# Fixed issue order, rescaling by halves with the third product two halves later, and splits dealt out, in a bilinear pair kernel

## The chip, the cores and the metric

The kernel runs on one core of one Trainium2 chip. Times are microseconds (us) of device time for one execution; the median of several runs is quoted. Engines are named as in the profile: PE is TensorE (matmuls), PEld its weight loads, DVE is VectorE, ACT is ScalarE, POOL is GpSimd, SP is SyncE, which issues the transfers.

## The reference

For each of the 496 pairs i < j of 32 fields, a 1024 x 128 slice of the input is multiplied by its own 128 x 128 matrix, and the result is multiplied element by element with field j:

```python
v_i = inputs[:, I_IDX, :]          # inputs: 1024 x 32 x 128, fp32
v_j = inputs[:, J_IDX, :]
transformed = jnp.einsum('bpd,ped->bpe', v_i, W)   # W: 496 x 128 x 128
return transformed * v_j           # 1024 x 496 x 128, fp32: 260 MB to write
```

## The kernel before

A pair's result stands in one PSUM tile of 128 x 1024 fp32, with two halves of 512 columns. Each half is one bank of PSUM (point (4) of the prediction's part on the Trainium skill). The first 15 pairs use plain fp32 matmuls. For the other 481, weights and inputs are split into a high and a low part, and the result is put together from three faster products: two are summed in PSUM (`wh*xh`, `wl*xl`; the *first products* below), ScalarE rescales the sum in place, and the *third product* (`wd*xd`) is added on top. VectorE then multiplies by field j, and SyncE sends the output tile off.

```python
LAG = 2
ppool = ctx.enter_context(tc.tile_pool(name="ps", bufs=4, space=bass.MemoryType.PSUM))
...
for q in range(NQ + LAG):
    if q < NQ:
        ...   # at the start of a group of four pairs: load weights, split weights two groups ahead
        ...   # at the start of a field: load an x, split the next field's x
        po[q] = ppool.tile([P, BT], F32, tag="po", name=f"po_{q}")
        ...
            for t in (0, 1):
                for h in range(0, BT, HB):
                    nc.tensor.matmul(po[q][:, h : h + HB], w_s[c][t][:, r], x_s[i][t][:, h : h + HB],
                                     start=t == 0, stop=t == 1)
            nc.scalar.mul(po[q], po[q], 1.0 + EPS)      # both halves at once
    if q >= LAG:
        ...   # third products of pair q - LAG, both halves
        ...   # VectorE's product of the whole pair, and the output's transfer
```

The layer that builds the program inserts all semaphore waits by itself. In the kernel before it also sorts each engine's instructions by its own estimate of time, so the order in the source is only a wish.

A split of four pairs' weights is one ScalarE instruction and three GpSimd ones (3.2 us on GpSimd); a split of half a field's x is the same.

Of the kernel before, what the change touches and what calls it, by code (L numbers as in the profile page):

```python
# [1 line left out]

# [4 lines left out]

F32 = mybir.dt.float32
F32R = mybir.dt.float32r
ALU = mybir.AluOpType  # L10

P = 128
NF = 32
NQ = NF * (NF - 1) // 2
BT = 1024
HB = 512
WC = 4
EPS = 2.0**-12
NATIVE = 5
LAG = 2  # L20


def _pairs():

    return [(i, j) for i in range(NF - 2, -1, -1) for j in range(i + 1, NF)]


@with_exitstack
def kernel(
    ctx: ExitStack,  # L30
    tc: tile.TileContext,
    xt: bass.AP,
    wt: bass.AP,
    out: bass.AP,
):
















    nc = tc.nc
    pairs = _pairs()
    nchunk = NQ // WC

    xpool = ctx.enter_context(tc.tile_pool(name="x", bufs=1))
    spool = ctx.enter_context(tc.tile_pool(name="xs", bufs=2))
    rpool = ctx.enter_context(tc.tile_pool(name="wr", bufs=4))
    wpool = ctx.enter_context(tc.tile_pool(name="ws", bufs=3))
    tpool = ctx.enter_context(tc.tile_pool(name="tmp", bufs=2))  # L60
    opool = ctx.enter_context(tc.tile_pool(name="o", bufs=6))
    ppool = ctx.enter_context(tc.tile_pool(name="ps", bufs=4, space=bass.MemoryType.PSUM))

    x_sb = {}

    def load_x(f, pieces=1):
        x_sb[f] = xpool.tile([P, BT], F32, tag=f"x{f}", name=f"x_{f}")
        s = BT // pieces
        for k in range(pieces):
            nc.sync.dma_start(out=x_sb[f][:, k * s : (k + 1) * s], in_=xt[:, f, k * s : (k + 1) * s])  # L70

    w_raw = {}

    def load_w(c, splits=(0, WC)):
        w_raw[c] = rpool.tile([P, WC, P], F32, tag="w", name=f"w_{c}")
        for a, b in zip(splits, splits[1:]):
            nc.sync.dma_start(out=w_raw[c][:, a:b, :], in_=wt[:, c * WC + a : c * WC + b, :])

    w_s = {}

    def split_w(c):

        raw = w_raw[c].rearrange("p q e -> p (q e)")
        h, l, d = [wpool.tile([P, WC * P], F32R, tag=t, name=f"{t}_{c}") for t in ("wh", "wl", "wd")]
        hs = tpool.tile([P, WC * P], F32, tag="t", name=f"whs_{c}")
        nc.scalar.mul(h, raw, 1.0 - 2.0**-13)  # L86
        nc.gpsimd.tensor_tensor(l, raw, h.bitcast(F32), ALU.subtract)  # L87
        nc.gpsimd.tensor_scalar(hs, h.bitcast(F32), EPS, 1.0, ALU.mult, ALU.mult)  # L88
        nc.gpsimd.tensor_tensor(d, l.bitcast(F32), hs, ALU.subtract)  # L89
        w_s[c] = (h, l, d)  # L90

    x_s = {}

    def split_x(f):

        h, l, d = [spool.tile([P, BT], F32R, tag=t, name=f"{t}_{f}") for t in ("xh", "xl", "xd")]
        for a in range(0, BT, HB):
            s = slice(a, a + HB)
            ls = tpool.tile([P, HB], F32, tag="t", name=f"xls_{f}_{a}")
            nc.scalar.mul(h[:, s], x_sb[f][:, s], 1.0 - 2.0**-13)  # L100
            nc.gpsimd.tensor_tensor(ls, x_sb[f][:, s], h[:, s].bitcast(F32), ALU.subtract)  # L101
            nc.gpsimd.tensor_scalar(l[:, s], ls, 1.0 / EPS, 1.0, ALU.mult, ALU.mult)  # L102
            nc.gpsimd.tensor_tensor(d[:, s], h[:, s].bitcast(F32), l[:, s].bitcast(F32), ALU.subtract)  # L103
        x_s[f] = (h, l, d)

    nq0 = NATIVE * (NATIVE + 1) // 2
    c0 = nq0 // WC

    load_w(0, (0, 1, WC))
    load_x(NF - 2, 2)  # L110
    load_x(NF - 1, 2)
    load_x(NF - 3)
    load_w(1)
    for f in (NF - 4, NF - 5):
        load_x(f)
    load_w(2)

    out_v = out.rearrange("q e b -> q e b")
    po = {}

    def finish(q):
        j = pairs[q][1]
        ot = opool.tile([P, BT], F32, tag="ot", name=f"ot_{q}")
        pieces = 2 if q >= NQ - 2 else 1
        s0 = BT // pieces
        for k in range(pieces):
            s = slice(k * s0, (k + 1) * s0)
            nc.vector.tensor_tensor(ot[:, s], po[q][:, s], x_sb[j][:, s], ALU.mult)  # L128
            nc.sync.dma_start(out=out_v[q, :, s], in_=ot[:, s])

    def second(q):
        i, _ = pairs[q]
        r = slice(q % WC * P, (q % WC + 1) * P)
        for h in range(0, BT, HB):
            nc.tensor.matmul(  # L135
                po[q][:, h : h + HB], w_s[q // WC][2][:, r], x_s[i][2][:, h : h + HB], start=False, stop=True,
                skip_group_check=True,
            )

    for q in range(NQ + LAG):  # L140
        if q < NQ:
            i, j = pairs[q]
            c = q // WC
            if q % WC == 0:
                if c + 3 < nchunk:
                    load_w(c + 3)
                for k in ([c + 2] if c > 0 else [0, 1, 2]):
                    if c0 <= k < nchunk:
                        split_w(k)
            if j == i + 1:  # L150
                for f in ([i - 4] if i < NF - 2 else [NF - 6]):
                    if f >= 0:
                        load_x(f)
                if 0 <= i - 1 < NF - 1 - NATIVE:
                    split_x(i - 1)
            po[q] = ppool.tile([P, BT], F32, tag="po", name=f"po_{q}")
            if q < nq0:
                for h in range(0, BT, HB):
                    nc.tensor.matmul(  # L159
                        po[q][:, h : h + HB],  # L160
                        w_raw[c][:, q % WC, :],
                        x_sb[i][:, h : h + HB],
                        start=True,
                        stop=True,
                    )
            else:
                r = slice(q % WC * P, (q % WC + 1) * P)
                for t in (0, 1):
                    for h in range(0, BT, HB):
                        nc.tensor.matmul(  # L170
                            po[q][:, h : h + HB],
                            w_s[c][t][:, r],
                            x_s[i][t][:, h : h + HB],
                            start=t == 0,
                            stop=t == 1,
                        )
                nc.scalar.mul(po[q], po[q], 1.0 + EPS)  # L177
        if q >= LAG:
            if q - LAG >= nq0:
                second(q - LAG)  # L180
            finish(q - LAG)


# [25 lines left out]
```

## Time and profile before

| | before |
|---|---|
| median of 4 runs | 898.5 us |
| span of the profiled run | 896.0 us |
| TensorE busy | 761.1 us, 85% |
| VectorE, ScalarE, GpSimd busy | 607.0, 558.2, 549.5 us |
| mean transfer rate | 346 GB/s |
| time per pair, 896 / 496 | 1.81 us |

Busy shares do not say who sets the pace; the waits and the order of time do. The lines are in the prediction below.

### The profile page before, as it was taken

How to read it: one execution, taken by the hardware profiler on the slowest of the kernel's cores; microseconds unless marked ns; L12 is line 12 of the kernel's file. 1: busy time of each engine (PE TensorE's matmuls, PEld its weight loads, DVE VectorE, ACT ScalarE, POOL GpSimd, SP SyncE). 2: the span in 40 equal slices, each digit the busy share in tenths (PEclk: the TensorE clock that was granted, in tenths of full speed). 3: DMA queues.
4: the chain of work that ended last, by engine and by line, in shares of the span. 5: the costliest groups of instructions: out<-in, count | busy, mean ns of one | idle time of the engine just before them, and what ended most of it. 6: DMA issues, size and time to landing. Idle time of an engine off the chain costs nothing.

```text
span 896.0 us, 10407 instructions
## 1 busy us (share of the span) xinstructions
PE 761.1 (85%) x2946; PEld 526.2 (59%) x2946; DVE 607.0 (68%) x498; ACT 558.2 (62%) x655; POOL 549.5 (61%) x523
## 2 busy tenths in 40 slices
PE   7988888888888888888888888888888888898887
PEld 2455555555666565555565666655656566665665
DVE  3666666666777666676676767776667777677766
ACT  2266666666676566566665667665756666666565
POOL 1878877777666774664747565665655647474441
PEclk9999999999999999999999999999999999999999
DMA  8999999899999898998998999998998899999997
GB/s 329 416 340 370 360 355 343 318 361 338 376 357 362 332 370 327 339 361 320 353 343 336 343 363 356 355 352 321 355 341 334 336 339 330 343 345 339 337 342 304
DMA packets 94666, 310.03 MB, mean 346 GB/s; under 512 B 10513, under 2 KB 10769, under 8 KB 94609
## 3 DMA queue, kind: packets, MB, share of 16 engines
q1 hardware_dynamic: 94608, 309.37, 92.3%
q8 instruction: 23, 0.38, 0.2%
q14 instruction: 35, 0.28, 0.1%
HBM read 49.28 MB, written 260.05 MB: 345 GB/s over the span
## 4 chain that ended last, share of the span: by engine, by line
PE 32%; ACT 25%; issue 19%; POOL 11%; DMA 1%; DVE 0%; POOLq 0%; ACTq 0%; DVEq 0%
ACT po L177 20%; PE po L170 17%; PE po L135 14%; ACT wh L86 4%; POOL wl L87 4%; POOL wd L89 4%; POOL whs L88 2%; DMA out_dram<-ot 1%; ACT xh L100 1%; POOL xls L101 1%; DVE ot L128 0%; POOL xl L102 0%; POOLq L87 0%; ACTq L177 0%; POOL xd L103 0%
## 5 line engine op out<-in xcount | busy, mean ns | idle before, releaser
L128 DVE TENSOR_TENSOR ot<-po,x 128x1024 f32<-128x1024 f32 (+1 forms) x498 | 607.0, 1220 | 285.4 <-ACT po L177 141.7
L177 ACT ACTIVATE po<-po 128x1024 f32<-128x1024 f32 x481 | 476.9, 1009 | 298.5 <-PE po L170 298.5
L135 PE MATMUL po<-xd,wd 128*128 128x512 f32 x962 | 325.7, 420 | 123.8 <-ACT po L177 123.0
L87 POOL TENSOR_TENSOR wl<-w,wh 128x512 fp32r<-128x512 f32 x121 | 154.5, 1277 | 301.7 <-ACT wh L86 301.7
L135 PEld LDWEIGHTS po<-xd,wd 128*128 128x128 f32 x962 | 152.7, 188 | 257.5 <-ACT po L177 162.8
L170 PE MATMUL po<-xh,wh 128*128 128x512 f32 x962 | 300.9, 394 | 0.0
L170 PE MATMUL po<-xl,wl 128*128 128x512 f32 x962 | 298.1, 391 | 0.0
L170 PEld LDWEIGHTS po<-xl,wl 128*128 128x128 f32 x962 | 180.6, 188 | 42.2
L170 PEld LDWEIGHTS po<-xh,wh 128*128 128x128 f32 x962 | 180.6, 188 | 42.1 <-issue 0.5
L89 POOL TENSOR_TENSOR wd<-wl,whs 128x512 fp32r<-128x512 f32 x121 | 156.6, 1294 | 7.9
L86 ACT ACTIVATE wh<-w 128x512 fp32r<-128x512 f32 x121 | 75.5, 624 | 19.3 <-DMA w<-in_wt_dram 19.3
L88 POOL TENSOR_SCALAR whs<-wh 128x512 f32<-128x512 f32 x121 | 75.1, 621 | 10.2
L101 POOL TENSOR_TENSOR xls<-x,xh 128x512 f32<-128x512 f32 x52 | 67.4, 1296 | 4.2
L103 POOL TENSOR_TENSOR xd<-xh,xl 128x512 fp32r<-128x512 f32 x52 | 66.9, 1287 | 2.2
L100 ACT ACTIVATE xh<-x 128x512 fp32r<-128x512 f32 x52 | 32.1, 621 | 13.6 <-PE po L170 8.7
L102 POOL TENSOR_SCALAR xl<-xls 128x512 fp32r<-128x512 f32 x52 | 32.4, 623 | 4.4
L159 PE MATMUL po<-x,w 128*128 128x512 f32 x60 | 29.6, 656 | 6.2 <-DMA x<-in_xt_dram 6.2
L159 PEld LDWEIGHTS po<-x,w 128*128 128x128 f32 x60 | 12.3, 209 | 22.6 <-issue 21.6
L86 ACT ACT_TABLE_LOAD x1 | 1.3, 1283 | 0.7 <-PEq L196 0.7
L196 POOL MEMSET const-float32-0.0<- 128x1 f32 x1 | 0.1, 99 | 0.2 <-issue 0.2
L196 POOL MEMSET const-bfloat16-1.0<- 128x1 bf16 x1 | 0.1, 102 | 0.0
L196 POOL MEMSET const-uint8-127<- 128x1 uint8 x1 | 0.1, 102 | 0.0
(1 smaller groups left out, 0.1 us busy)
## 6 DMA issues: line engine op xcount, KB each, us to landing
out_dram<-ot SPq DMA_DIRECT2D x494, 512.0 KB, 3.8
w<-in_wt_dram SPq DMA_DIRECT2D x123, 256.0 KB, 3.9
x<-in_xt_dram SPq DMA_DIRECT2D x30, 512.0 KB, 6.0
x<-in_xt_dram SPq DMA_DIRECT2D x4, 256.0 KB, 4.4
out_dram<-ot SPq DMA_DIRECT2D x4, 256.0 KB, 2.6
w<-in_wt_dram SPq DMA_DIRECT2D x1, 192.0 KB, 2.6
w<-in_wt_dram SPq DMA_DIRECT2D x1, 64.0 KB, 1.8
```

What stands on the lines that cost most here:

```text
L86: nc.scalar.mul(h, raw, 1.0 - 2.0**-13)
L87: nc.gpsimd.tensor_tensor(l, raw, h.bitcast(F32), ALU.subtract)
L88: nc.gpsimd.tensor_scalar(hs, h.bitcast(F32), EPS, 1.0, ALU.mult, ALU.mult)
L89: nc.gpsimd.tensor_tensor(d, l.bitcast(F32), hs, ALU.subtract)
L100: nc.scalar.mul(h[:, s], x_sb[f][:, s], 1.0 - 2.0**-13)
L101: nc.gpsimd.tensor_tensor(ls, x_sb[f][:, s], h[:, s].bitcast(F32), ALU.subtract)
L103: nc.gpsimd.tensor_tensor(d[:, s], h[:, s].bitcast(F32), l[:, s].bitcast(F32), ALU.subtract)
L128: nc.vector.tensor_tensor(ot[:, s], po[q][:, s], x_sb[j][:, s], ALU.mult)
L135: nc.tensor.matmul(po[q][:, h : h + HB], w_s[q // WC][2][:, r], x_s[i][2][:, h : h + HB], start=False, stop=True, skip_group_check=True,)
L159: nc.tensor.matmul(po[q][:, h : h + HB], w_raw[c][:, q % WC, :], x_sb[i][:, h : h + HB], start=True, stop=True,)
L170: nc.tensor.matmul(po[q][:, h : h + HB], w_s[c][t][:, r], x_s[i][t][:, h : h + HB], start=t == 0, stop=t == 1,)
L177: nc.scalar.mul(po[q], po[q], 1.0 + EPS)
```

## The change

Its intent is to end the turns that TensorE and ScalarE take. One context manager fixes each engine's order as the source has it. The unit becomes half a pair: two products of half u, its rescaling, then the third product of half u - 2. VectorE still multiplies whole pairs. Splits are put on a list with an earliest and a latest pair, and at most one is issued per pair. Output tiles go from 6 to 5, raw weight tiles from 4 to 5, and the first two x tiles are issued from ScalarE.

```diff
+    ctx.enter_context(tc.manual_schedule())
+    def first(u):
+        q, h = divmod(u, 2)
+        ...
+        s = slice(h * HB, (h + 1) * HB)
+        if h == 0:
+            po[q] = ppool.tile([P, BT], F32, tag="po", name=f"po_{q}")
+        ...
+            for t in (0, 1):
+                nc.tensor.matmul(po[q][:, s], w_s[c][t][:, r], x_s[i][t][:, s], start=t == 0, stop=t == 1)
+            nc.scalar.mul(po[q][:, s], po[q][:, s], 1.0 + EPS)
+    def second(u):
+        ...
+            nc.tensor.matmul(
+                po[q][:, s], w_s[q // WC][2][:, r], x_s[i][2][:, s], start=False, stop=True, skip_group_check=True
             )
+        ...
+        elif h == 1:
+            nc.vector.tensor_tensor(ots[q], po.pop(q), x_sb[j], ALU.mult)
+            nc.sync.dma_start(out=out[q], in_=ots[q])
+    for u in range(2 * NQ + LAG):
+        ...
+            first(u)
+        if u >= LAG:
+            second(u - LAG)
+        if u % 2 == 1:
+            ready = [t for t in todo if t[0] <= q]
+            if ready:
+                ready[0][2]()
+                todo.remove(ready[0])
```

(The removed lines are those of the kernel before, above.)

More of the change, by code (lines that the diff above doesn't have):

```diff
@@ L20 @@
 LAG = 2
+WLEAD = 4
+XLEAD = 3
 def _pairs():
@@ L57, with load_x @@
     spool = ctx.enter_context(tc.tile_pool(name="xs", bufs=2))
-    rpool = ctx.enter_context(tc.tile_pool(name="wr", bufs=4))
+    rpool = ctx.enter_context(tc.tile_pool(name="wr", bufs=5))
     wpool = ctx.enter_context(tc.tile_pool(name="ws", bufs=3))
     tpool = ctx.enter_context(tc.tile_pool(name="tmp", bufs=2))
-    opool = ctx.enter_context(tc.tile_pool(name="o", bufs=6))
+    opool = ctx.enter_context(tc.tile_pool(name="o", bufs=5))
     ppool = ctx.enter_context(tc.tile_pool(name="ps", bufs=4, space=bass.MemoryType.PSUM))
     x_sb = {}
-    def load_x(f, pieces=1):
+    def load_x(f, pieces=1, eng=None):
         x_sb[f] = xpool.tile([P, BT], F32, tag=f"x{f}", name=f"x_{f}")
@@ L69, in load_x @@
         for k in range(pieces):
-            nc.sync.dma_start(out=x_sb[f][:, k * s : (k + 1) * s], in_=xt[:, f, k * s : (k + 1) * s])
+            (eng or nc.sync).dma_start(out=x_sb[f][:, k * s : (k + 1) * s], in_=xt[:, f, k * s : (k + 1) * s])
     w_raw = {}
@@ L92, with split_x @@
     x_s = {}
-    def split_x(f):
-        h, l, d = [spool.tile([P, BT], F32R, tag=t, name=f"{t}_{f}") for t in ("xh", "xl", "xd")]
-        for a in range(0, BT, HB):
-            s = slice(a, a + HB)
-            ls = tpool.tile([P, HB], F32, tag="t", name=f"xls_{f}_{a}")
-            nc.scalar.mul(h[:, s], x_sb[f][:, s], 1.0 - 2.0**-13)
-            nc.gpsimd.tensor_tensor(ls, x_sb[f][:, s], h[:, s].bitcast(F32), ALU.subtract)
-            nc.gpsimd.tensor_scalar(l[:, s], ls, 1.0 / EPS, 1.0, ALU.mult, ALU.mult)
-            nc.gpsimd.tensor_tensor(d[:, s], h[:, s].bitcast(F32), l[:, s].bitcast(F32), ALU.subtract)
-        x_s[f] = (h, l, d)
+    def split_x(f, a):
+        if a == 0:
+            x_s[f] = [spool.tile([P, BT], F32R, tag=t, name=f"{t}_{f}") for t in ("xh", "xl", "xd")]
+        s = slice(a, a + HB)
+        h, l, d = [t[:, s] for t in x_s[f]]
+        ls = tpool.tile([P, HB], F32, tag="t", name=f"xls_{f}_{a}")
+        nc.scalar.mul(h, x_sb[f][:, s], 1.0 - 2.0**-13)
+        nc.gpsimd.tensor_tensor(ls, x_sb[f][:, s], h.bitcast(F32), ALU.subtract)
+        nc.gpsimd.tensor_scalar(l, ls, 1.0 / EPS, 1.0, ALU.mult, ALU.mult)
+        nc.gpsimd.tensor_tensor(d, h.bitcast(F32), l.bitcast(F32), ALU.subtract)
@@ L106 @@
     nq0 = NATIVE * (NATIVE + 1) // 2
     c0 = nq0 // WC
+    first_q = {i: q for q, (i, j) in reversed(list(enumerate(pairs)))}
+    todo = []
+    for c in range(c0, nchunk):
+        todo.append(((c - 2) * WC + 1, max(c * WC, nq0), lambda c=c: split_w(c)))
+    for i in range(NF - 2 - NATIVE, -1, -1):
+        for a in range(0, BT, HB):
+            todo.append((first_q[i + 1] + 1 if i < NF - 3 - NATIVE else 2, first_q[i], lambda i=i, a=a: split_x(i, a)))
+    todo.sort(key=lambda t: t[1])
     load_w(0, (0, 1, WC))
-    load_x(NF - 2, 2)
@@ L111 @@
-    load_x(NF - 1, 2)
+    load_x(NF - 2, 2, nc.scalar)
+    load_x(NF - 1, 2, nc.scalar)
     load_x(NF - 3)
     load_w(1)
-    for f in (NF - 4, NF - 5):
+    for f in range(NF - 4, NF - 4 - XLEAD, -1):
         load_x(f)
-    load_w(2)
-    out_v = out.rearrange("q e b -> q e b")
-    po = {}
-    def finish(q):
-        j = pairs[q][1]
-        ot = opool.tile([P, BT], F32, tag="ot", name=f"ot_{q}")
-        pieces = 2 if q >= NQ - 2 else 1
-        s0 = BT // pieces
-        for k in range(pieces):
-            s = slice(k * s0, (k + 1) * s0)
-            nc.vector.tensor_tensor(ot[:, s], po[q][:, s], x_sb[j][:, s], ALU.mult)
-            nc.sync.dma_start(out=out_v[q, :, s], in_=ot[:, s])
@@ L131, in second @@
-    def second(q):
-        i, _ = pairs[q]
-        r = slice(q % WC * P, (q % WC + 1) * P)
-        for h in range(0, BT, HB):
+    for c in range(2, WLEAD):
+        load_w(c)
+    ctx.enter_context(tc.manual_schedule())
+    po, ots = {}, {}
+    def first(u):
+        q, h = divmod(u, 2)
+        i, c = pairs[q][0], q // WC
+        r = slice(q % WC * P, (q % WC + 1) * P)
+        s = slice(h * HB, (h + 1) * HB)
+        if h == 0:
+            po[q] = ppool.tile([P, BT], F32, tag="po", name=f"po_{q}")
+        if q < nq0:
+            nc.tensor.matmul(po[q][:, s], w_raw[c][:, q % WC, :], x_sb[i][:, s], start=True, stop=True)
+        else:
+            for t in (0, 1):
+                nc.tensor.matmul(po[q][:, s], w_s[c][t][:, r], x_s[i][t][:, s], start=t == 0, stop=t == 1)
+            nc.scalar.mul(po[q][:, s], po[q][:, s], 1.0 + EPS)
@@ L135, in second @@
+    def second(u):
+        q, h = divmod(u, 2)
+        i, j = pairs[q]
+        r = slice(q % WC * P, (q % WC + 1) * P)
+        s = slice(h * HB, (h + 1) * HB)
+        if q >= nq0:
             nc.tensor.matmul(
-                po[q][:, h : h + HB], w_s[q // WC][2][:, r], x_s[i][2][:, h : h + HB], start=False, stop=True,
-                skip_group_check=True,
-            )
-    for q in range(NQ + LAG):
-        if q < NQ:
-            i, j = pairs[q]
-            c = q // WC
-            if q % WC == 0:
-                if c + 3 < nchunk:
-                    load_w(c + 3)
-                for k in ([c + 2] if c > 0 else [0, 1, 2]):
-                    if c0 <= k < nchunk:
-                        split_w(k)
-            if j == i + 1:
-                for f in ([i - 4] if i < NF - 2 else [NF - 6]):
-                    if f >= 0:
-                        load_x(f)
-                if 0 <= i - 1 < NF - 1 - NATIVE:
-                    split_x(i - 1)
-            po[q] = ppool.tile([P, BT], F32, tag="po", name=f"po_{q}")
-            if q < nq0:
-                for h in range(0, BT, HB):
-                    nc.tensor.matmul(
-                        po[q][:, h : h + HB],
-                        w_raw[c][:, q % WC, :],
-                        x_sb[i][:, h : h + HB],
-                        start=True,
-                        stop=True,
-                    )
-            else:
-                r = slice(q % WC * P, (q % WC + 1) * P)
-                for t in (0, 1):
-                    for h in range(0, BT, HB):
-                        nc.tensor.matmul(
-                            po[q][:, h : h + HB],
-                            w_s[c][t][:, r],
-                            x_s[i][t][:, h : h + HB],
-                            start=t == 0,
-                            stop=t == 1,
-                        )
-                nc.scalar.mul(po[q], po[q], 1.0 + EPS)
-        if q >= LAG:
-            if q - LAG >= nq0:
-                second(q - LAG)
-            finish(q - LAG)
@@ new lines, in second @@
+                po[q][:, s], w_s[q // WC][2][:, r], x_s[i][2][:, s], start=False, stop=True, skip_group_check=True
+            )
+        if h == 0:
+            ots[q] = opool.tile([P, BT], F32, tag="ot", name=f"ot_{q}")
+        if q >= NQ - 2:
+            nc.vector.tensor_tensor(ots[q][:, s], po[q][:, s], x_sb[j][:, s], ALU.mult)
+            nc.sync.dma_start(out=out[q, :, s], in_=ots[q][:, s])
+        elif h == 1:
+            nc.vector.tensor_tensor(ots[q], po.pop(q), x_sb[j], ALU.mult)
+            nc.sync.dma_start(out=out[q], in_=ots[q])
@@ new lines @@
+    for u in range(2 * NQ + LAG):
+        q = u // 2
+        if u % (2 * WC) == 0 and q // WC + WLEAD < nchunk:
+            load_w(q // WC + WLEAD)
+        if u < 2 * NQ:
+            i, j = pairs[q]
+            if u % 2 == 0 and j == i + 1 and 0 <= i - 2 - XLEAD:
+                load_x(i - 2 - XLEAD)
+            first(u)
[6 more added lines that the diff above has]
+                todo.remove(ready[0])
@@ L184 @@
+    assert not todo
 def kernel(**inputs):
```

## The prediction

> **What bounds the kernel now.** I read the page's busy table first, for the engine nearest to its limit, then the waits of every engine, then the order of time within four pairs, and last the DMA rate in stretches where the queue was full.
>
> ```profile
> PE 761.1 (85%) x2946; PEld 526.2 (59%) x2946; DVE 607.0 (68%) x498; ACT 558.2 (62%) x655; POOL 549.5 (61%) x523
> ...
> q1 hardware_dynamic: 94608, 309.37, 92.3%
> ```
>
> No engine is full. The DMA engines look it at 92%, but that is the time that packets were under way; the bytes decide, below. PE's 761 us is not solid either, because ends of matmuls are modelled. From the starts in the trace, two neighbouring 512-column matmuls lie 232 ns apart (median), so the six of a pair need 6 x 0.232 = 1.39 us. A pair takes 896 / 496 = 1.81 us. Who waits for whom:
>
> ```profile
> ACT po L177 <- PE po L170: 298.5, 237, 7.8
> PEld po L135 <- ACT po L177: 162.8, 195, 1.7
> DVE ot L128 <- ACT po L177: 141.7, 89, 1.6
> PE po L135 <- ACT po L177: 123.0, 245, 1.2
> ```
>
> TensorE waits for ScalarE's rescaling of the pair, and ScalarE waits for TensorE: they take turns. The order of time shows how:
>
> ```profile
> 402.34 0.62 PE L170 MATMUL po<-xh,wh 128*128 128x512 f32 x2
> 402.80 0.62 PE L170 MATMUL po<-xl,wl 128*128 128x512 f32 x2
> ...
> 403.26 0.62 PE L170 MATMUL po<-xh,wh 128*128 128x512 f32 x2
> 403.46 1.01 ACT L177 ACTIVATE po<-po 128x1024 f32<-128x1024 f32 x1 [1.75 <-PE po L170]
> 403.72 0.61 PE L170 MATMUL po<-xl,wl 128*128 128x512 f32 x2
> 404.38 0.62 ACT L86 ACTIVATE wh<-w 128x512 fp32r<-128x512 f32 x1
> 404.52 0.73 PE L135 MATMUL po<-xd,wd 128*128 128x512 f32 x2 [0.19 <-ACT po L177]
> ...
> 404.91 1.02 ACT L177 ACTIVATE po<-po 128x1024 f32<-128x1024 f32 x1
> ...
> 405.97 0.74 PE L135 MATMUL po<-xd,wd 128*128 128x512 f32 x2 [0.72 <-ACT po L177]
> ...
> 406.55 0.62 PE L170 MATMUL po<-xh,wh 128*128 128x512 f32 x2
> ```
>
> The source asks for a lag of two pairs, but the built order here is the first two products of pairs A and B, then the third products of A and B at once. TensorE therefore waits for A's rescaling, and for B's behind a weight split (404.38) that sits between the two. Eight first products, four third ones and their waits take 406.55 - 402.34 = 4.21 us instead of 2.78. This comes once in each group of four pairs: of the 497 gaps between starts of VectorE's products, 334 lie between 1.35 and 1.50 us (TensorE's own pace), and 125 between 2.4 and 3.0, beside 121 weight splits. The long ones cost about 125 x (2.82 - 1.40) = 178 us. Summing TensorE's start-to-start gaps beyond the normal 232 ns gives 203 us, of which 187 are before third products.
>
> Then the transfers:
>
> ```profile
> 20.00:40.00 20.00, 19.75 (x53) 9.58 (x51) 13.48 (x11) 4.38 (x7) 16.97 (x17) 1.00 1.03 417
> 180.00:190.00 10.00, 8.39 (x35) 5.84 (x34) 7.41 (x7) 6.59 (x8) 9.50 (x10) 1.00 1.03 417
> 300.00:400.00 100.00, 85.57 (x338) 60.02 (x338) 68.31 (x56) 63.79 (x76) 62.40 (x60) 1.00 0.92 343
> 430.00:440.00 10.00, 8.40 (x34) 5.83 (x34) 7.58 (x7) 6.27 (x8) 9.50 (x10) 1.00 1.03 418
> ```
>
> The last column is GB/s. With enough outputs outstanding the queue moves 417, also in 1 us slices with no load under way and two to four outputs outstanding (419). On average it moves 346. So a share of 0.92 hides a sixth of spare rate, and the kernel is bound by the turns of TensorE and ScalarE, with the DMA limit 17% below.
>
> **What the Trainium skill says.** (1) "ScalarE: Activation LUTs", section "What ACT_TABLE_LOAD costs": an ACTIVATE with immediate scale takes 186 ns + 0.833 ns per element, and neighbours overlap by about 93 ns. The trace agrees closely: 624 ns at 512 columns (613 by the formula), 1009 at 1024 in PSUM (1039), and two of the latter back to back take 1.93 us, 0.09 less than twice one. (2) "DMA: Bandwidth & Descriptors", "Specifications": 435 GB/s at the fabric, about 358 from HBM for each core. The trace holds 417 for 20 us, so 358 is not the limit on this core. (3) "TensorE: Matmul & The Clock Gate", the table at its head: matmuls keep program order and ScalarE's queue is strictly first in, first out, so an instruction placed badly holds all behind it. The split at 404.38 does just that. (4) "PSUM — Partial Sum Buffer", "Terms": a bank holds 512 fp32, so half of a pair is one bank, and ScalarE can rescale one while TensorE writes the other. No run shows that yet.
>
> **The change, part by part.** *Half-wise work, third product two halves later.* TensorE does two matmuls of half u, then the third of u-2. After the first two of u end, five matmuls pass (u+1's two, u-1's third, u+2's two) before u's third: 5 x 0.232 = 1.16 us. A half's rescaling is estimated at 1.009 - 512 x 0.833 ns = 0.58, at most 0.62 as in the splits. So 0.5 us of slack is left in every half, and the 187 us of waits before third products should go. One split (0.62) in front delays a half to about 0.1 us before or after its deadline, and the surplus of 0.70 - 0.58 per half recovers that.
>
> *Price on ScalarE.* 481 rescalings of 1009 ns become 962 of about 0.60: 577 instead of 477 us; with splits (75.5 + 32.1) 685 us less overlaps of up to 0.09 each. Per pair at most 1.42 us: it comes near TensorE's 1.39 but lies beside it.
>
> *VectorE by whole pairs*: as before, 1.22 us per pair. *Splits dealt out*, at most one per pair, about seven pairs ahead: the same 173 GpSimd jobs of some 3.2 us, 549 us in all, off the path except early, where the groups of the first field are short: 7 to 9 pairs need four jobs, 12.7 us, and TensorE takes 10 to 13. I expect 2 to 5 us of waits there and at the first weight splits.
>
> *Start*: two x tiles are issued from ScalarE while SyncE issues the rest; before, TensorE sat 1.60 us waiting for the third tile and DMA moved only 216 GB/s between 4 and 6 us. Gain 2 to 3 us. *Outputs 6 to 5 buffers*: four can be in flight while VectorE fills one, enough for the full rate seen with three. *Raw weights 4 to 5, one chunk more lead*: no cost on the path.
>
> The sum: TensorE alone would end at 30 (native pairs, 15 x 1.71 from 4.5) + 481 x 1.39 + 5 of tail = 704 us. Bytes: 310.03 MB / 0.417 = 743, plus 2.5 us before the first byte and about 3 of ramp and landing at the end: 749. The transfers take over as the bound: 1.50 us per pair on average, 1.45 late, where each field's x serves more pairs. TensorE and ScalarE lie so close to it (1.39, 1.42) that jitter will not be absorbed wholly by five output tiles and four PSUM tiles; I add 1%, 8 us. So 757 us, 141 less.
>
> **The rivals.** *A: five outputs starve the DMA.* An output lands 3.5 us (median) after issue, up to 5.5 when full; five slots at 1.5 us allow 7.5 per round: 1.22 for VectorE, 0.4 for the issue, 5.8 in flight. It fits; if it did not, some 1.6 us per pair, about 800. *B: ScalarE becomes the bound* through strict order: a split that waits for a raw weight, or a rescaling of 0.62 and no overlap, gives 1.46 plus waits, about 765 to 790. For it: 92% busy. Against: raw weights are loaded seven pairs before their split. *C: halves serialise*, if TensorE's write of one half had to wait for ScalarE's of the other in the same tile. Then each pair would gain two waits of some 0.6 us: 900 to 1000. Against: the second half of the first x tile is waited for separately in the trace (1.05 us before the third native weight load), so dependencies are kept by region. *D: the DMA doesn't hold 417 over the whole run* with mostly writes; at 400, 780. Nothing in the saturated stretches hints at it.
>
> **Range and chances.** The floor of 743 to 749 from bytes is hard, so the low end is 740; A, B or D half true give 795. Only C, or an unforeseen stall in the fixed order, would keep the time near 898. Faster by over 2%: 0.96; within 2%: 0.03; slower: 0.01.
>
> **What would show it.** Right: DMA near 410 to 418 GB/s in nearly all slices; VectorE waiting for output tiles to land; waits of third products for ScalarE nearly gone; gaps between VectorE starts around 1.45 to 1.55 without the group at 2.8; ScalarE near 670 us busy with halves at 0.58 to 0.62. Wrong: DMA below 390 with TensorE waiting for ScalarE (B), for PSUM (C), or VectorE waiting for landings at a DMA rate well under 417 (A, D).

## The result, and the profile after

| | before | changed |
|---|---|---|
| median of 4 runs | 898.5 us | 1116.9 us |
| ratio, 95% interval | | 1.2435 (1.2414 to 1.2457) |
| span | 896.0 us | 1114.9 us |
| mean transfer rate | 346 GB/s | 278 GB/s |

Ratios are the mean time of one kernel's runs over that of the other's in the same rounds, so they differ a little from the quotient of the medians. The change made the kernel 24% slower.

In the changed kernel L148 holds the first products, L149 the rescaling, L157 the third product and L166 VectorE's; in other runs these numbers shift by a few lines. From its page, the busy times, the transfers and two groups (mean ns of one after the busy us, then idle time before them and what ended it):

```profile
PE 954.5 (86%) x2946; PEld 515.9 (46%) x2946; DVE 607.6 (54%) x498; ACT 637.9 (57%) x1136; POOL 549.3 (49%) x523
...
q1 hardware_dynamic: 94032, 308.32, 73.1%
...
L149 ACT ACTIVATE po<-po 128x512 f32<-128x512 f32 x962 | 560.9, 583 | 452.0 <-PE po L148 431.7
L148 PE MATMUL po<-xh,wh 128*128 128x512 f32 x962 | 430.6, 448 | 121.1 <-ACT po L149 86.8
```

The transfers, which should have become the bound, are emptier than before. ScalarE is busy 80 us longer, as the halves cost, but idle 43% of the time: so it is not simply overloaded. TensorE's busy time rose although it does the same 2946 matmuls: a record lasts 0.39 to 0.50 us, its end is modelled, and in a stream with a pitch of 0.23 us records overlap, while the last one before a wait counts in full. The waits of the changed kernel, in us in total, times, longest:

```profile
ACT po L149 <- PE po L148: 431.7, 478, 10.4
PEld po L148 <- ACT po L149: 272.2, 481, 1.1
PEld po L157 <- ACT po L149: 172.2, 364, 0.8
PE po L148 <- ACT po L149: 86.8, 167, 0.7
```

Before, of TensorE's work only third products waited for ScalarE in the list. Now L148 does, the *first* products, 481 times: once in each pair, and never in the design. In order of time, one pair's period (start, duration, what; in brackets the idle time before it and what ended it):

```profile
406.20 0.19 PEld L148 LDWEIGHTS po<-xh,wh 128*128 128x128 f32 x1 [0.45 <-ACT po L149]
406.20 0.51 PE L148 MATMUL po<-xh,wh 128*128 128x512 f32 x1
...
406.55 0.39 PE L148 MATMUL po<-xl,wl 128*128 128x512 f32 x1
...
406.77 0.39 PE L157 MATMUL po<-xd,wd 128*128 128x512 f32 x1
...
407.00 0.39 PE L148 MATMUL po<-xh,wh 128*128 128x512 f32 x1
...
407.03 1.20 ACT L149 ACTIVATE po<-po 128x512 f32<-128x512 f32 x2 [0.88 <-PE po L148]
...
407.23 0.39 PE L148 MATMUL po<-xl,wl 128*128 128x512 f32 x1
407.67 0.19 PEld L157 LDWEIGHTS po<-xd,wd 128*128 128x128 f32 x1 [0.47 <-ACT po L149]
...
408.29 0.19 PEld L148 LDWEIGHTS po<-xh,wh 128*128 128x128 f32 x1 [0.43 <-ACT po L149]
```

At 406.20 TensorE starts the second half of pair q, then (406.77) a third product of q - 1, then the first half of q + 1 (407.00, 407.23). The last of these is over at 407.62. ScalarE's two rescalings, of q's second half and q + 1's first, end at 408.23. Only at 408.29 do the products of q + 1's second half begin. They write another bank, but they waited for that rescaling. The loop adds up: 407.23 - 406.20 = 1.03 for four starts, 0.39 for the last matmul to its end, about 0.60 for one rescaling, 0.06 to the restart: 2.08 us, against 1.39 without waits.

The built program says the same. Of pair 144, its instructions with the waits that the build put on them (a listing, not the profile; h0 and h1 are the halves; a wait is shown by the instruction that it waits for):

```
PE   first  h0   waits for VectorE's product of pair 140 (the tile's last user)
ACT  scale  h0   waits for PE first h0
PE   first  h1   waits for ACT scale h0      <- another bank, same tile
ACT  scale  h1   waits for ACT scale h0 (and for PE first h1)
PE   third  h0   waits for ACT scale h1      <- another bank, same tile
DVE  whole pair  waits for PE third h1
```

Both marked waits are between instructions that touch different halves. In the build used here, dependencies in a PSUM tile are kept by the whole tile. The listing is not kept with the runs, but the semaphores in the traces agree: the first weight load of a second half carries a wait on ScalarE's semaphore in all 481 pairs of the changed kernel, in 2 of e1 (a tile for each half) and in 1 of e3 (one rescaling for each pair).

Of the gaps between VectorE's starts, 312 average 2.10 us and 171 average 2.49; from the 21st product on, each of the 165 long ones holds exactly one of ScalarE's 173 splits, and the short ones none. A split thus adds 0.39 us to the loop, in front of the rescaling that TensorE waits for. 312 x 2.10 + 171 x 2.49 = 1081 of the 1115 us; the rest is the start and the plain fp32 pairs.

### The profile page after: what moved, and what is told of

The parts are those of the page before. It is cut to its first block, busy times and chain, and to the rows that moved or that the text cites. A ratio compares the mean times of both kernels' runs of the same rounds, so it can differ in the third digit from the quotient of the medians.

```text
span 1114.9 us, 11346 instructions
## 1 busy us (share of the span) xinstructions
PE 954.5 (86%) x2946; PEld 515.9 (46%) x2946; DVE 607.6 (54%) x498; ACT 637.9 (57%) x1136; POOL 549.3 (49%) x523
## 4 chain that ended last, share of the span: by engine, by line
PE 53%; ACT 34%; issue 10%; DMA 2%; ACTq 0%; DVE 0%; SPq 0%
PE po L148 44%; ACT po L149 25%; PE po L157 7%; ACT wh L88 6%; ACT xh L103 3%; PE po L145 2%; DMA x<-in_xt_dram 1%; DMA out_dram<-ot 1%; ACTq L149 0%; DVE ot L166 0%; SPq L167 0%; DVE ot L163 0%; SPq L79 0%
## 5 line engine op out<-in xcount | busy, mean ns | idle before, releaser
L166 DVE TENSOR_TENSOR ot<-po,x 128x1024 f32<-128x1024 f32 x494 | 604.9, 1225 | 503.1 <-PE po L157 484.2
L149 ACT ACTIVATE po<-po 128x512 f32<-128x512 f32 x962 | 560.9, 583 | 452.0 <-PE po L148 431.7
L148 PE MATMUL po<-xh,wh 128*128 128x512 f32 x962 | 430.6, 448 | 121.1 <-ACT po L149 86.8
L157 PE MATMUL po<-xd,wd 128*128 128x512 f32 x962 | 426.2, 443 | 30.6 <-ACT po L149 1.8
L148 PE MATMUL po<-xl,wl 128*128 128x512 f32 x962 | 380.0, 395 | 0.0
L148 PEld LDWEIGHTS po<-xh,wh 128*128 128x128 f32 x962 | 179.8, 187 | 294.2 <-ACT po L149 272.2
L157 PEld LDWEIGHTS po<-xd,wd 128*128 128x128 f32 x962 | 180.0, 187 | 258.4 <-ACT po L149 172.2
L148 PEld LDWEIGHTS po<-xl,wl 128*128 128x128 f32 x962 | 181.1, 188 | 20.9 <-issue 0.2
L163 DVE TENSOR_TENSOR ot<-po,x 128x512 f32<-128x512 f32 x4 | 2.7, 689 | 1.3 <-PE po L157 1.3
```

The source lines that it names most:

```text
L148: nc.tensor.matmul(po[q][:, s], w_s[c][t][:, r], x_s[i][t][:, s], start=t == 0, stop=t == 1)
L149: nc.scalar.mul(po[q][:, s], po[q][:, s], 1.0 + EPS)
L157: nc.tensor.matmul(po[q][:, s], w_s[q // WC][2][:, r], x_s[i][2][:, s], start=False, stop=True, skip_group_check=True)
L166: nc.vector.tensor_tensor(ots[q], po.pop(q), x_sb[j], ALU.mult)
```

## The experiments

Theory S: the halves serialise, because they share a tile. Rivals: B, ScalarE is the bound with its 962 rescalings in strict order; O, the fixed order with dealt splits is itself the cost. The medians, each with the ratio to the kernel before in the same rounds:

| run | what differs | us | ratio |
|---|---|---|---|
| changed kernel | | 1116.9 | 1.2435 |
| e1 | one PSUM tile for each half, VectorE by halves | 779.2 | 0.8675 |
| e2 | VectorE by halves only | 1137.6 | 1.2665 |
| e3 | one rescaling per pair, third product 3 halves later | 775.3 | 0.8630 |
| e4 | halves of two pairs interleaved | 867.5 | 0.9658 |
| e5 | kernel before, halves only | 1086.1 | 1.2092 |
| e6 | e3 with the third product 2 halves later | 1039.1 | 1.1568 |
| e7 | e3 with splits at their old places | 772.3 | 0.8598 |
| e8 | e3 with the old buffers (six output tiles) | 776.9 | 0.8646 |
| e9 | changed kernel, third product 3 halves later | 1115.8 | 1.2423 |
| e10 | e3 without the fixed order | 939.4 | 1.0458 |
| e11 | e7 with the old buffers | 776.4 | 0.8643 |

All are correct. e1 to e4 ran on one chip, e5 to e8 and e9 to e11 together as well.

### e1: a tile for each half

```diff
-    ppool = ctx.enter_context(tc.tile_pool(name="ps", bufs=4, space=bass.MemoryType.PSUM))
+    ppool = ctx.enter_context(tc.tile_pool(name="ps", bufs=8, space=bass.MemoryType.PSUM))
-        if h == 0:
-            po[q] = ppool.tile([P, BT], F32, tag="po", name=f"po_{q}")
+        po[u] = ppool.tile([P, HB], F32, tag="po", name=f"po_{u}")
-            nc.scalar.mul(po[q][:, s], po[q][:, s], 1.0 + EPS)
+            nc.scalar.mul(po[u], po[u], 1.0 + EPS)
+        nc.vector.tensor_tensor(ots[q][:, s], po[u], x_sb[j][:, s], ALU.mult)
```

(The matmuls' `po[q][:, s]` becomes `po[u]` too.)

> Edit: each half has its own one-bank PSUM tile (8 instead of 4), VectorE multiplies by halves[...]; order, splits and buffers as in the changed kernel. Theory S (the halves serialise: the two halves share one tile, and the built program makes TensorE wait for ScalarE's last rescaling of the OTHER half of that tile): those waits go, the 2.1 us per pair fall to the transfers' 1.5, 750 to 800 us. Rival B (ScalarE, with twice as many rescalings in strict order, is the bound): the number of rescalings is the same, so 1050 to 1120. Rival O (the fixed order itself, with splits dealt out, is the cost): order is the same, so 1050 to 1120.

It took 779.2 us, 13% faster than the kernel before. It issues as many rescalings in the same order, so B and O fall. Nor is it the finer freeing of PSUM by eight tiles: in the changed kernel's list TensorE's first products never wait for VectorE. Apart from GpSimd's, the longest waits of e1 are of another kind:

```profile
PEld po L147 <- DVE ot L161: 88.7, 142, 3.6
ACT po L148 <- PE po L147: 81.4, 119, 7.7
DVE ot L161 <- DMA out_dram<-ot: 63.8, 73, 3.8
```

VectorE waits for output tiles to land, and TensorE for VectorE to free PSUM: the transfers hold everything back, as the prediction had it for the change itself.

### e2: the control for e1

```diff
-        elif h == 1:
-            nc.vector.tensor_tensor(ots[q], po.pop(q), x_sb[j], ALU.mult)
+        nc.vector.tensor_tensor(ots[q][:, s], po[q][:, s], x_sb[j][:, s], ALU.mult)
```

> Control for e1: the changed kernel with VectorE by halves and nothing else (whole-pair PSUM tiles stay). Theory S: no gain, 1110 to 1200, since the third product of the second half now also waits for VectorE's product of the first. If VectorE by halves were what helps e1, this one would be fast too, under 900.

1137.6 us. VectorE by halves alone makes it worse, by a third wait of the same kind: the second half's third product waits for VectorE's product of the first half (all 481 carry a wait on VectorE's semaphore). So e1's gain is that of the tiles.

```profile
PEld po L157 <- DVE ot L162: 96.0, 298, 1.5
```

### e3: one rescaling for each pair

```diff
-LAG = 2
+LAG = 3
-            nc.scalar.mul(po[q][:, s], po[q][:, s], 1.0 + EPS)
+            if h == 1:
+                nc.scalar.mul(po[q], po[q], 1.0 + EPS)
```

> Edit: the changed kernel with one rescaling per pair (1024 columns, after the second half's products) and the third product three halves later instead of two; tiles, order, VectorE, splits stay. Theory S: with one rescaling per tile there is nothing to wait for in the other half, so TensorE keeps its 1.39 us per pair and the transfers bound: 750 to 800 us. Rival B: also faster (477 instead of 561 us busy), so this run does not tell S from B; e1 does. Rival O: stays above 1050.

775.3 us, with the tiles and the fixed order of the changed kernel. If the rescaling covers the tile, a wait for the whole tile is no loss. Three stretches of e3, with busy time by engine, then granted clock, share of transfers and GB/s in the last columns:

```profile
100.00:200.00 100.00, 93.53 (x384) 68.10 (x383) 78.23 (x64) 76.20 (x90) 84.75 (x81) 1.00 1.02 403
300.00:400.00 100.00, 95.81 (x396) 70.74 (x397) 81.04 (x67) 76.23 (x89) 72.67 (x69) 1.00 1.02 405
500.00:600.00 100.00, 96.39 (x403) 71.36 (x403) 82.17 (x68) 77.34 (x90) 68.03 (x64) 1.00 1.02 405
```

Compare the stretch from 300 to 400 us of the kernel before in the prediction: 343 GB/s at a share of 0.92. Here the share is 1.02, and the median time from the end of an output's issue to its landing is 5.4 us instead of 3.5: the queue is full all along.

### e4: the same instructions, another order

```diff
-LAG = 2
+LAG = 3
+    halves = [2 * (q + b) + h for q in range(0, NQ, 2) for h in (0, 1) for b in (0, 1)]
...
+            u = halves[p]
             first(u)
...
+            second(halves[p - LAG])
```

> Edit: only the order of the halves: first halves of two pairs, then their second halves, third product three halves later; the same instructions, tiles and number of rescalings as the changed kernel. Theory S: the other half's rescaling (0.6 us) now has another pair's 0.7 us of products to hide behind, so most of the wait goes: 760 to 850 us. Rival B: the same load on ScalarE, so no gain, above 1050.

867.5 us: tiles and instructions unchanged, 249 us less, so again not B (the lag of three alone changes nothing, e9). It missed its range by 17 us. A part of the wait remains, and a new one came:

```profile
PEld po L148 <- DVE ot L166: 82.1, 237, 2.1
PEld po L157 <- ACT po L149: 81.6, 230, 0.7
PEld po L148 <- ACT po L149: 45.4, 253, 0.6
```

L148's wait for ScalarE is down from 272 to 45 us. But two pairs are open at once, and with four tiles TensorE now waits 237 times for VectorE to free one.

### e5: the halves alone, in the kernel before

```diff
-                for t in (0, 1):
-                    for h in range(0, BT, HB):
+                for h in range(0, BT, HB):
+                    for t in (0, 1):
                         nc.tensor.matmul(...)
-                nc.scalar.mul(po[q], po[q], 1.0 + EPS)
+                    nc.scalar.mul(po[q][:, h : h + HB], po[q][:, h : h + HB], 1.0 + EPS)
```

> Edit: the kernel BEFORE with products and rescaling by halves (1024-column rescaling cut in two, third products still in the old built order); nothing else of the change. Theory S: the halves alone cost, whatever fixes the order: a pair gains the same two waits for the other half, 950 to 1150 us. If halves were harmful only in the fixed order, it would stay at 880 to 910.

1086.1 us, 21% slower than before, in the sorted order too. But the expectation that the third products keep the old built order did not hold: eight first products followed by four third ones stand 114 times in the kernel before and 5 times here. So the order changed with the halves, and the run does not isolate them; 467 of the 481 second halves' first weight loads do carry the wait on ScalarE's semaphore.

### e6: how much later the third product must come

> Edit: e3 with the third product two halves later, as in the changed kernel, instead of three. Between the end of a pair's products and its third product TensorE then has three matmuls, 0.70 us; the rescaling of 1024 columns needs 0.09 + 1.01 + 0.06 = 1.16. Wait of 0.46 per pair, 1.85 us per pair: 880 to 950 us. It says how much of e3's gain needs the third half; if about 775, the lag does not matter.

1039.1 us, 89 above its range: the lag matters more than I had worked out. The edit is `LAG = 2` in e3. The order of time shows the missing part:

```profile
401.29 0.50 PE L158 MATMUL po<-xd,wd 128*128 128x512 f32 x1 [0.41 <-ACT po L150]
...
401.62 0.40 PE L148 MATMUL po<-xh,wh 128*128 128x512 f32 x1
...
401.86 0.39 PE L148 MATMUL po<-xl,wl 128*128 128x512 f32 x1
...
402.29 1.01 ACT L150 ACTIVATE po<-po 128x1024 f32<-128x1024 f32 x1 [0.52 <-PE po L148]
```

I had counted matmuls at their pitch of 0.23 us. But after a wait the second matmul starts 0.33 us after the first, and the last one, which a waiter waits for, takes 0.39 from start to end. The loop is 0.33 + 0.24 + 0.39 + 0.04 + 1.01 and 0.05 to 0.14 to the restart, 2.06 to 2.15 us in place of 1.85. 472 of its 497 gaps between VectorE starts lie between 2.0 and 2.2.

### e7: splits where they were

> Edit: e3 with each split written where the kernel before writes it (at the start of its group of four pairs or of its field, both halves of x together) instead of dealt out one per pair after the buffer is free. The split then stands in ScalarE's queue before its buffer's last reader, a third product three halves later: ScalarE stands still some 1.1 us, and the rescaling behind it comes 1.4 us late, once in four pairs: 860 to 920 us. If the dealing out is worth nothing: 770 to 785.

772.3 us, and no loss at all. The edit takes out the list and calls `split_w(q // WC + 2)` and `split_x(i - 1, a)` ahead of `first(u)`, at the start of a group or field. My expectation was wrong in its premise: the last reader of the high part that ScalarE overwrites is a *first* product, not the third (which reads only the difference part that GpSimd writes), so nothing holds ScalarE; in e7's waits no split waits for TensorE. Dealing the splits out is worth nothing here. This is the fastest kernel, 14% faster than the kernel before.

### e8 and e11: output tiles

> Edit: e3 with the buffers of the kernel before: six output tiles, four raw weight tiles, weights three groups ahead. Transfers bound e3 at 400 GB/s with outputs landing 5.4 us after issue. If five output tiles still starve the DMA a little (rival A of the prediction), 755 to 768; if the DMA is full, 770 to 778.

> Edit: e7 with e8's buffers (six output tiles, four raw weight tiles, three groups ahead), as a candidate for the fastest. Both are bound by the transfers at about 402 GB/s over the span; nothing is left to hide, so 766 to 774 us. Under 760 would say that output tiles still limited e7.

776.9 and 776.4 us (e11 is 2 us above its range): a sixth output tile does not help (e3 has 775.3, e7 772.3), so there is no sign that five starve the transfers. The edits set 6 output tiles, 4 raw weight tiles and `WLEAD = 3`; the last two came along, to keep the memory that the kernel before uses, so a small gain of the sixth tile that they cancel is not excluded.

### e9: which of the two waits sets the pace

> Edit: the changed kernel with the third product three halves later instead of two; halves still share a tile. It takes the wait of the first half's third product for the second half's rescaling off (that rescaling has three more matmuls to hide behind) and leaves the wait of the second half's products for the first half's rescaling. If the latter alone sets the pace (first half's products 0.7 with their drain, 0.09, rescaling 0.58, 0.06, second half's products 0.57, third product 0.23 in between: about 2.1 us per pair), nothing moves: 1080 to 1130. If the third product's wait sets it: 850 to 980.

1115.8 us, as the changed kernel to 0.1%. The edit is `LAG = 3`. The waits:

```profile
PEld po L148 <- ACT po L149: 484.9, 481, 1.6
...
PE po L148 <- ACT po L149: 278.4, 481, 1.1
```

L157, the third product, no longer waits for ScalarE anywhere in the list, and L148 waits more instead. So the pace is set by the second half's products waiting for the first half's rescaling; the other wait only filled the same time.

### e10: the fixed order

> Edit: e3 with the one line that fixes the order taken out, so that the build sorts each engine's instructions by its own estimate again; e3's source order, lag, dealt splits and buffers stay. The built order again has the products of two pairs followed by both third products. If the fixed order is what e3 gains over the kernel before: 860 to 920 us. If the order as written in the source (lag of three halves, dealt splits) is enough: 770 to 800.

939.4 us: 21% slower than e3 by one removed line, and 5% slower than the kernel before; 19 us outside the range. In the built order, two pairs' first products again stand ahead of both pairs' third products, 117 times (114 in the kernel before). ScalarE also stands before weight splits, where the kernel before has no such wait in its list:

```profile
ACT wh L88 <- PE po L147: 171.3, 101, 10.9
```

That this makes e10 slower than the kernel before is not tested. The fixed order is the part of the change that was worth having: 164 us in e3. It is not enough alone, since e6 has it too. The kernel before with the fixed order and nothing else was not run.

## Why the prediction was wrong

- **What bounds the kernel before** (TensorE and ScalarE taking turns, with 17% of transfer rate to spare): right, with 14% to spare by the 402 GB/s that e7 kept up. e3 fixes the order and keeps the rest of the work, and goes to 775.3 us with full transfers; e10 gives the gain back.
- **Half-wise work leaves 0.5 us of slack in every half: this is the step that failed.** It counted the third product's own rescaling as the only wait. The built program has two more for each pair, and one of them sets the pace: the second half's products wait for the first half's rescaling, in all 481 pairs, and a pair takes 2.10 us instead of 1.39 (e9 has only this wait and the same time). It was written down as rival C and set aside on the ground that "dependencies are kept by region", which the trace had shown for an x tile in SBUF. In PSUM it does not hold. The inference went from one memory to another without a sign from the second.
- **Rival C's size**, 900 to 1000 us, was too low, and its sum does not give it. Two waits of 0.6 us on top of 1.39 are 2.59 a pair, 1281 us by the prediction's own sum (30 + 481 x 2.59 + 5); one such wait gives 992. What the runs show is one wait that sets the pace, but a longer one: the loop of 2.10 us also holds the last matmul's 0.39 us and the slow restart, and 171 pairs have a split in it at 0.39 more.
- **The price on ScalarE**, 577 us of rescaling: 560.9 measured (583 ns each). Right, and beside the point.
- **Splits off the path**: wrong in the changed kernel, where they cost 171 x 0.39 = 67 us, because ScalarE is in the loop. Dealing them out gave nothing (e7).
- **The start**, 2 to 3 us gained: not seen. VectorE's first product starts at 11.0 us in the changed kernel and at 8.4 in the one before.
- **The transfers as the new bound, 757 us**: wrong for the change, but where the false waits are gone (e1, e3, e7) it comes out at 772 to 779. The size is off by the rate: 403 to 405 GB/s in the full stretches of e3, where 417 was taken from stretches of the kernel before. The prediction's support for 417, 419 in 1 us slices with two to four outputs outstanding and no load under way, does not come out of the trace: the 75 slices that fit average 366 GB/s (385 in 66 slices, if an output counts from the end of its issue). Why a full queue stays below 417 over long stretches is open. Loads of x account for part of it at most: in 1 us slices of e3 with 3.5 to 4 outputs outstanding it moved 386 GB/s on average with such a load under way (118 slices) and 406 without (411).
- **Rivals A and B**: both off; e8 gives no sign of A and e1 shows B wrong. D, a lower rate over the whole run, was right once the waits are gone: it said 780 us at 400 GB/s, and e3 took 775.3 at 400.

## What to carry to other kernels

Before cutting an instruction into pieces so that two engines can overlap within a tile, look in the built program at what each piece waits for; if dependencies are kept by the tile, make the pieces separate tiles, or keep one instruction per tile. Here, evidence of fine dependencies in one memory did not carry over to another. Count a loop through a wait with the latency of its last matmul and the restart, not with the pitch of a stream: that alone was 0.2 to 0.3 us of 2.1 in e6.

## What the Trainium skill lacked or had wrong

- No page has it: in the build used here, dependencies in a PSUM tile are kept by the whole tile, even between halves in different banks. "PSUM — Partial Sum Buffer" (Terms) says that the danger is two engines in the same bank; here the halves lie in different banks and still wait. Measured: 1116.9 us with a shared tile, 779.2 with a tile per half (e1; its control e2, with a shared tile, 1137.6).
- "TensorE: Matmul & The Clock Gate", section "Back-to-back issue gap", gives 216 ns for 512 columns, and 131 sustained. Here the median is 232 ns in the kernel before, and after a wait the second matmul starts 330 to 350 ns after the first.
- "DMA: Bandwidth & Descriptors", "Specifications", gives about 358 GB/s from HBM for each core. The page itself explains, under "Measured", that a core alone reads up to 425, so this is no error; what it lacks is a figure for a mix of mostly writes. This kernel, on one core, moved 402 GB/s over its whole span in e7, 84% of it writes.
- "ScalarE: Activation LUTs", "What ACT_TABLE_LOAD costs": its formula gives 613 ns at 512 columns; the rescaling from PSUM to PSUM took 583 (the splits, from SBUF to SBUF, 623). The page does say that PSUM is the faster destination, but not by how much.
